# Graph layer kernel on one core: values and queries of layer 0 as seven block products

## The chip, the cores and the metric

The kernel runs on one NeuronCore of a Trainium2 chip. The core has five engines, each with its own instruction stream: TensorE (matmuls and its weight loads; PE and PEld in the profile), VectorE (DVE), ScalarE (ACT), GpSimd (POOL) and SyncE (SP), which here only starts transfers. They meet through semaphores. Matmul results land in PSUM, eight banks of 2 KB per partition; the rest of the working data is in SBUF, 128 partitions wide. The metric is the device time of one execution in microseconds (us), as the median of several runs.

## The reference

Two layers over 4096 rows of 512 features. Only the head of layer 0 is touched by the change:

```python
h = relu(layernorm(x))                       # 4096 x 512
q = h @ Wq.T + bq;  k = h @ Wk.T + bk;  v = h @ Wv.T + bv
a = q @ k.T / sqrt(512) + adj + adj
x = x + softmax(a) @ v
# layer 1: a graph attention with 8 heads on relu(layernorm(x)), and x + elu(...)
```

Everything is fp32 in layer 0. The kernel never forms k: q k.T is h (Wq.T Wk) h.T plus a bias term, so it forms A = Wq.T Wk once, then "queries" h A + c for each block of rows, and multiplies those with h.

## The kernel before, in words

*Stages.* In the profiled execution the projection runs from 0 to about 273 us, then the attention of layer 0 up to about 1.86 ms, a short preparation, and layer 1. In the attention stages matmuls are already written as seven products of half-size blocks (Strassen's scheme in Winograd's form) instead of eight: `product` and `weighted` with factors named A11 to A22, S1 to S4 (sums of blocks of h) and B11 to B22, T1 to T4 (sums of blocks of the other side). The projection before multiplies in the plain way.

*The projection* goes over eight blocks of 512 rows (NS = 8, `sb` in the code). For a block:

- `load_x` fetches four tiles of 128 rows; `normalize` (VectorE) takes means and variances, asks GpSimd for a power (`inverse_root`, L168), refines it in four small steps and scales the four tiles.
- `hidden` turns the block: 16 transposes on TensorE into two PSUM banks (tag `pt`), four activations on ScalarE (L411) into `hT`, then four sums on GpSimd into `hS` (L419 to L422; S1 to S4), and stores of both for the attention stage.
- `values_of`: for each of four tiles of 128 rows, four matmuls of 512 columns into one PSUM bank (L433), and one sum with the bias on VectorE into `v` (L437). Then per pair of tiles four GpSimd operations (L442 to L445) that make the sums T1, T2, T3 and T4 of `v`, T2 in place.
- `queries`: for each of four column blocks o of A, four matmuls of 512 columns into one bank (L459), one VectorE operation that adds c, scales by half_scale and reorders into `qs` (L463). Then four GpSimd sums (L472 to L475) and seven stores to `q_d`, in the order B21, B11, T1, T2, B22, T3, T4.

Both kinds of matmul take their bank from one tag, `mm`, with four banks.

*Order.* `seq` (`keep_in_program_order`) keeps every engine in the order in which the code names its instructions. In round sb that is: `normalize(sb + 1)`, `values_of(sb)`, `hidden(sb + 1)`, in round 2 `center_weights` (six VectorE operations, L252 to L254), in rounds 3 to 6 `weigh_weights` (four GpSimd products L260, each with a VectorE reduction L265), then `queries(sb)`. So on VectorE the sums of `values_of(sb)` stand behind `normalize(sb + 1)`, and on GpSimd the power of `normalize(sb + 1)` stands behind the query sums of round sb - 1. Round 0 is written out before the loop: loads of x, of Wv (L492), of Wq and Wk (`load_blocks`, L318), `normalize(0)`, `hidden(0)`, bias loads from ScalarE (L499, L500), eight VectorE transposes of Wq and Wk (L324), `values_of(0)`, `normalize(1)`, `attention_vectors` (small VectorE work for layer 1, L211 to L232), a GpSimd product of Wk with the bias (L507), 16 matmuls `pa` for A (L513) with ScalarE copies into `a_sb` (L517), the reduction to `c_sb` (L518), `hidden(1)`, `queries(0)`.

*Space.* `early` holds the 11 buffers of tag `qt` for query factors; `bv_sb` takes one during the projection. At round 6, `load_chunk(0)` loads seven.

Of the kernel before, what the change touches and what calls it, by code (L numbers as in the profile page):

```python
# [10 lines left out]
F32 = mybir.dt.float32  # L11
BF16 = mybir.dt.bfloat16
AF = mybir.ActivationFunctionType
ALU = mybir.AluOpType
# [65 lines left out]
def fast_path(  # L80
# [29 lines left out]
    def sources_of_rows(t):  # L110

        return t.rearrange("p (q c r) -> p c q r", c=SB, r=R)
# [195 lines left out]
    with tc.tile_pool(name="early", bufs=2) as early, tc.tile_pool(name="kv", bufs=1) as kv:  # L308
# [68 lines left out]
        with tc.tile_pool(name="proj_c", bufs=1) as pc, tc.tile_pool(  # L377
            name="proj", bufs=2
        ) as work, tc.tile_pool(name="proj_ps", bufs=2, space=PSUM) as psum:

            wv_sb = [
                pc.tile([P, D], F32, name=f"wv{k}_sb") for k in range(KC)
            ]
            a_sb = pc.tile([P, KC, D], F32, name="a_sb")
            c_sb = pc.tile([P, KC], F32, name="c_sb")
            bv_sb = early.tile([P, D], F32, name="bv_sb", tag="qt", bufs=11)
# [18 lines left out]
            def hidden(sb, xt):  # L405
# [20 lines left out]
                flat = "p a b c d -> p (a b c d)"  # L426
                seq(nc.sync.dma_start(out=s_d[sb].rearrange(flat), in_=sums.rearrange(flat)))

            def values_of(sb):
                for b in range(SB):  # L430
                    pv = psum.tile([P, 512], F32, name="pv", tag="mm", bufs=4)
                    for k in range(KC):
                        seq(nc.tensor.matmul(  # L433
                            pv, hidden_of[sb][0][:, k, ts(b, P)], wv_sb[k],
                            start=k == 0, stop=k == KC - 1,
                        ))
                    seq(nc.vector.tensor_add(v[:, sb * SB + b, :], pv, bv_sb))  # L437
                for pair in range(SB // 2):
                    one, two = v[:, sb * SB + 2 * pair, :], v[:, sb * SB + 2 * pair + 1, :]
                    b11, b12, b21, b22 = one[:, 0:H], one[:, H:D], two[:, 0:H], two[:, H:D]  # L440
                    t = early.tile([P, 3, H], F32, name="tv", tag="tv", bufs=2)
                    seq(nc.gpsimd.tensor_sub(t[:, 0], b12, b11))  # L442
                    seq(nc.gpsimd.tensor_sub(t[:, 1], b22, b12))
                    seq(nc.gpsimd.tensor_sub(b12, b22, t[:, 0]))
                    seq(nc.gpsimd.tensor_sub(t[:, 2], b21, b12))  # L445
                    seq(nc.sync.dma_start(
                        out=vt_d[sb * (SB // 2) + pair].rearrange("p f d -> p (f d)"),
                        in_=t.rearrange("p f d -> p (f d)"),
                    ))
# [3 lines left out]

            def queries(sb):
                qs = pc.tile([P, KC, GC], F32, name="qs", tag="qs", bufs=1)
                for o in range(KC):
                    pq = psum.tile([P, 512], F32, name="pq", tag="mm", bufs=4)
                    for k in range(KC):
                        seq(nc.tensor.matmul(  # L459
                            pq, a_sb[:, k, ts(o, P)], hidden_of[sb][0][:, k, :],  # L460
                            start=k == 0, stop=k == KC - 1,
                        ))
                    seq(nc.vector.tensor_scalar(  # L463
                        sources_of_rows(qs[:, o, :]), pq.rearrange("p (c q r) -> p c q r", c=SB, r=R),
                        c_sb[:, o : o + 1], half_scale, ALU.add, ALU.mult,
                    ))
                ts4 = prep.tile([P, SB, KC // 2, H], F32, name="ts4", tag="x1", bufs=1)
                t = [ts4[:, e] for e in range(4)]
                b = {f"{k + 1}{i + 1}": qs[:, 2 * k : 2 * k + 2, ts(i, H)]
                     for i in range(2) for k in range(2)}  # L470

                seq(nc.gpsimd.tensor_sub(t[0], b["12"], b["11"]))  # L472
                seq(nc.gpsimd.tensor_sub(t[1], b["22"], t[0]))
                seq(nc.gpsimd.tensor_sub(t[2], b["22"], b["12"]))
                seq(nc.gpsimd.tensor_sub(t[3], b["21"], t[1]))  # L475
                for f, name in enumerate(FACTORS):
                    seq(nc.sync.dma_start(
                        out=q_d[sb, :, f], in_=b[name[1:]] if name[0] == "B" else t[int(name[1]) - 1]
                    ))
# [9 lines left out]

            xts = {0: load_x(0)}  # L490
            for k in range(KC):
                seq(nc.sync.dma_start(out=wv_sb[k], in_=wvT[ts(k, P), :]))  # L492
            load_blocks(raw["q"], wqT)
            load_blocks(raw["k"], wkT)
            xts[1] = load_x(1)
            seq(nc.sync.dma_start(out=wk_rows, in_=wkT.rearrange("(k p) o -> p k o", p=P)))
            normalize(xts[0])
            hidden(0, xts.pop(0))
            seq(nc.scalar.dma_start(out=bv_sb, in_=bv[None, :].to_broadcast([P, D])))  # L499
# [8 lines left out]
                wk_rows, wk_rows, bq_sb.unsqueeze(1).to_broadcast([P, KC, D])  # L508
            ))
            for k in range(KC):  # L510
                pa_ps = psum.tile([P, 512], F32, name="pa", tag="mm", bufs=4)
                for c in range(SB):
                    seq(nc.tensor.matmul(  # L513
                        pa_ps, turned["q"][:, c, ts(k, P)], turned["k"][:, c, :],
                        start=c == 0, stop=c == SB - 1,
                    ))
                seq(nc.scalar.copy(a_sb[:, k, :], pa_ps))  # L517
            seq(nc.vector.tensor_reduce(c_sb, wk_rows, AX.X, ALU.add))  # L518
            xts[2] = load_x(2)
            hidden(1, xts[1])  # L520
            queries(0)
# [1223 lines left out]
```

## Time and profile before

| | |
|---|---|
| median of three runs | 3674.54 us (3672.04 to 3674.67) |
| the profiled execution's own time | 3674.76 us |
| its span, first to last instruction | 3672.7 us |
| mean granted TensorE clock | 0.988 of full |
| busy: TensorE / VectorE / GpSimd / ScalarE | 97% / 69% / 62% / 48% |
| projection stage | 0 to about 273 us |
| one round of it (95.16 to 125.03 us) | 29.87 us |

How to read the rows below: a line in order of time has start (us), duration (us), engine, line of the kernel, operation, output <- input (buffer numbers left out), shape, and xN for N merged instructions; in square brackets the time that the engine sat idle before it and what released it. PE matmul durations are pipelined: 592 ns is shown for a 512-column pass, while passes start 0.429 us apart, so times between starts are used. An fp32 matmul is recorded as two passes.

### The profile page before, as it was taken

The numbers are of one execution on the slowest core, as the hardware profiler recorded it, in microseconds if no ns is written. First come the engines' busy times: TensorE is split into PE (matmuls) and PEld (weight loads), VectorE is DVE, ScalarE is ACT, GpSimd is POOL, SyncE is SP. The second block draws the span as 40 slices with busy tenths as digits, with TensorE's granted clock in tenths as the row PEclk, the third lists the DMA queues.
The fourth block names the chain that finished last, engine by engine and source line by source line (L and its number), as shares of the span: only waits on it lengthen the run. The fifth ranks groups of instructions, "written<-read, shape, count | busy, mean of one in ns | idle before, by whom it ended". The sixth has DMA issues, their size and how long they took to land. (4 is left out here: it accounts for less than half of the span.)

```text
span 3672.7 us, 58831 instructions
## 1 busy us (share of the span) xinstructions
PE 3551.3 (97%) x21482; PEld 2084.0 (57%) x21482; DVE 2548.8 (69%) x4195; ACT 1745.0 (48%) x1541; POOL 2263.0 (62%) x1770
## 2 busy tenths in 40 slices
PE   8998999999999999999988799999999999999998
PEld 3447888888888888888866223322222223322332
DVE  5435565666666665656556678888888888888887
ACT  1000111111111111111123589998999999989997
POOL 4653445454545454444445568887888888877886
PEclk9999999999999999999999899999999999999999
DMA  6567788888888888888758987887787787778775
GB/s 213 180 207 203 230 242 239 238 242 244 237 234 250 237 237 243 241 249 232 217 143 207 214 220 211 211 212 201 211 209 212 203 213 204 209 198 214 211 210 151
DMA packets 667530, 796.85 MB, mean 217 GB/s; under 512 B 86816, under 2 KB 489696, under 8 KB 658016
## 3 DMA queue, kind: packets, MB, share of 16 engines
q1 hardware_dynamic: 655136, 759.64, 73.6%
q0 software_dynamic: 10704, 31.98, 4.8%
q8 instruction: 171, 2.80, 0.3%
q10 hardware_dynamic: 1392, 1.38, 0.1%
q14 instruction: 127, 1.04, 0.1%
HBM read 602.28 MB, written 182.71 MB: 214 GB/s over the span
## 5 line engine op out<-in xcount | busy, mean ns | idle before, releaser
L928 POOL TENSOR_TENSOR t<-t,g 128x1024 f32<-128x1024 f32 x512 | 1223.1, 2398 | 318.0 <-DVE t L922 242.4
L947 PE MATMUL acc<-t,nX 128*64 128x512 f32 x4096 | 1009.9, 609 | 0.0
L935 ACT ACTIVATE t<-t 128x2048 f32<-128x2048 f32 (+1 forms) x527 | 976.6, 1854 | 0.2 <-POOL t L928 0.2
L922 DVE SCALAR_TENSOR_TENSOR t<-u,at2m,r 128x512 f32<-128x512 f32 x1024 | 718.6, 743 | 209.3 <-issue 145.3
L597 ACT ACTIVATE aT<-aT 128x512 f32<-128x512 f32 x256 | 161.2, 630 | 1415.7 <-DVE aT L593 1415.7
L593 DVE TENSOR_TENSOR aT<-aT,XZ 128x256 f32<-128x256 f32 x896 | 352.9, 417 | 596.8 <-PE XZ L585 592.4
L931 DVE TENSOR_TENSOR t<-l,g 128x1024 f32<-128x1024 f32 x512 | 622.5, 1216 | 20.7 <-DMA g<-gT_d 16.7
L890 ACT ACTIVATE l<-l 128x1024 f32<-128x1024 f32 x512 | 516.5, 1009 | 149.4 <-PE l L884 101.5
L947 PEld LDWEIGHTS acc<-t,nX 128*64 128x64 f32 x4096 | 248.0, 136 | 458.3 <-issue 450.7
L585 PE MATMUL XZ<-qt,hS 128*128 128x256 f32 x2048 | 488.2, 382 | 9.6 <-DVE aT L593 9.6
L585 PEld LDWEIGHTS XZ<-qt,hS 128*128 128x128 f32 x2048 | 390.6, 191 | 64.1 <-DVE aT L593 11.1
L609 POOL TENSOR_TENSOR S<-aT 128x256 f32<-128x256 f32 x128 | 93.0, 726 | 525.8 <-ACT aT L597 525.8
L585 PE MATMUL XZ<-qt,hT 128*128 128x256 f32 x1536 | 374.3, 380 | 4.6 <-DVE aT L593 3.8
L621 POOL TENSOR_TENSOR total<-total,aT 128x256 f32<-128x256 f32 x360 | 326.5, 919 | 9.4
L585 PEld LDWEIGHTS XZ<-qt,hT 128*128 128x128 f32 x1536 | 291.3, 190 | 47.9 <-DVE aT L593 7.2
L874 PEld LDWEIGHTS <-z 6*128 6x128 bf16 x2048 | 52.4, 91 | 433.1 <-DVE t L922 350.2
L610 POOL TENSOR_TENSOR aT<-aT 128x256 f32<-128x256 f32 x128 | 93.0, 726 | 287.3 <-ACT aT L597 287.3
L636 PE MATMUL M<-v,aT 128*128 128x256 f32 x1024 | 263.0, 379 | 0.0
L636 PE MATMUL M<-tv,aT 128*128 128x256 f32 x1024 | 262.7, 379 | 0.0
L636 PE MATMUL M<-v,S 128*128 128x256 f32 x1024 | 242.0, 379 | 0.0
L577 DVE SCALAR_TENSOR_TENSOR gs<-ng,aT 128x512 f32<-128x512 bf16 x256 | 225.7, 882 | 8.8
L884 PE MATMUL l<-z_left,z 64*64 64x512 bf16 x2048 | 203.0, 383 | 26.8 <-DVE t L931 17.1
(178 smaller groups left out, 4372.0 us busy)
## 6 DMA issues: line engine op xcount, KB each, us to landing
g<-gT_d SPq DMA_DIRECT2D x128, 1024.0 KB
ag<-in_adj_dram SPq DMA_DIRECT2D x256, 256.0 KB
hS<-s_d SPq DMA_DIRECT2D x64, 1024.0 KB
gT_d<-gs SPq DMA_DIRECT2D x256, 256.0 KB
nb<-nT_d SPq DMA_DIRECT2D x128, 512.0 KB
nx<-nT_d SPq DMA_DIRECT2D x256, 256.0 KB
hT<-h_d SPq DMA_DIRECT2D x64, 768.0 KB
tv<-vt_d SPq DMA_DIRECT2D x128, 384.0 KB
```

The costliest lines, as they stand in the source:

```text
L577: seq(nc.vector.scalar_tensor_tensor(gs, ng, G_MASKED / NEG_BIG, aT, ALU.mult, ALU.add))
L585: seq(nc.tensor.matmul(out, a, b, start=start and k == 0, stop=k == 1, skip_group_check=not start,))
L593: seq(nc.vector.tensor_add(p, p, part))
L621: seq(nc.gpsimd.tensor_add(t, t, a))
L636: seq(nc.tensor.matmul(sums[ic][i][:, u, :], a[:, ts(u, P)], b, start=jt == 0 and u == 0, stop=jt == NB - 2, skip_group_check=u == 1,))
L884: seq(nc.tensor.matmul(lefts[n][ts(c, HD), r, :], loads[n // JB][2][ts(r, HD), jt % JB * P + c * HD :][:, :HD], groups[ic, hg]["z1_left"][ ...
L890: seq(nc.scalar.activation(lefts[n], lefts[n], AF.Relu, scale=4.0))
L922: seq(nc.vector.scalar_tensor_tensor(t[:, 2 + e, :], u4[:, e, :], at2m[:, jt, h : h + 1], right[e], ALU.max, ALU.add))
L928: seq(nc.gpsimd.tensor_mul(t[:, 2:4, :], t[:, 2:4, :], both_heads(n)))
L931: seq(nc.vector.tensor_mul(logits[n][:, 0:2, :], lefts.pop(n), both_heads(n)))
L935: seq(nc.scalar.activation(t, t, AF.Exp))
L947: seq(nc.tensor.matmul(grp["acc"][hf][ts(e, HD), :], nX[jt // SB][:, jt % SB, hg * HG + 2 * hf + e, :], t[:, hf + 2 * e, :], start=jt == 0 ...
```

## The change

The projections of values and of queries are written as seven products of half-size blocks, by the scheme that the attention stages use. A block of h (512 rows x 512 features) is cut into A11 to A22 by rows (even and odd tiles of 128, so the halves j) and by features (halves k); the sums S1 to S4 are those that `hidden` already makes for the attention stage. The weight (Wv, and A) is cut into B11 to B22. `weight_sums` forms T1, T3 and T4 of a weight in three new tiles and T2 in place of B12, with four GpSimd operations, once for each weight: for Wv right after the loads are issued, ahead of the first `normalize`; for A after the reduction to `c_sb`, ahead of `hidden(1)`.

`seven` runs four stages (`STAGES`). Each product is done in two halves u (values: tiles of 128 rows; queries: 128 output columns), and each half is a group of two matmuls of 256 columns. Tags X and Z have two banks each, one for each u. X is started once and accumulates X = A11 B11, then S2 T2, S3 T3 and A22 T4; Z is started anew in stages 0 and 1 and accumulates S4 B22 in stage 2. After every group VectorE reads the bank and adds it to the output's quarter: the first read of a quarter adds the bias, later ones add to what is there. Z of stage 0 with X of stage 0 gives quarter 11; Z of stage 1 starts quarter 22, X of stage 1 quarter 12; stage 2 completes 12 and 22; stage 3 gives 21. So a call has 28 matmuls of 256 columns and 14 VectorE operations of 256 columns, where it had 16 matmuls and 4 operations of 512. For queries, half_scale moves into `a_sb` (the ScalarE copy becomes a scaled one) and `c_sb` (one more small VectorE operation). The matmuls `pa` take their banks from X and Z in turn. The three tiles of sums of A come from the tag `qt`.

```diff
--- before.py
+++ after.py
@@ -378,9 +378,7 @@
             name="proj", bufs=2
         ) as work, tc.tile_pool(name="proj_ps", bufs=2, space=PSUM) as psum:
 
-            wv_sb = [
-                pc.tile([P, D], F32, name=f"wv{k}_sb") for k in range(KC)
-            ]
+            wv_sb = pc.tile([P, KC, D], F32, name="wv_sb")
             a_sb = pc.tile([P, KC, D], F32, name="a_sb")
             c_sb = pc.tile([P, KC], F32, name="c_sb")
             bv_sb = early.tile([P, D], F32, name="bv_sb", tag="qt", bufs=11)
@@ -426,15 +424,69 @@
                 flat = "p a b c d -> p (a b c d)"
                 seq(nc.sync.dma_start(out=s_d[sb].rearrange(flat), in_=sums.rearrange(flat)))
 
+            def weight_sums(w, tiles):
+
+                b11, b12, b21, b22 = [
+                    w[:, 2 * k : 2 * k + 2, ts(i, H)] for k in range(2) for i in range(2)
+                ]
+                t1, t3, t4 = tiles
+                seq(nc.gpsimd.tensor_sub(t1, b12, b11))
+                seq(nc.gpsimd.tensor_sub(t3, b22, b12))
+                seq(nc.gpsimd.tensor_sub(b12, b22, t1))
+                seq(nc.gpsimd.tensor_sub(t4, b21, b12))
+                return {"B11": b11, "B21": b21, "B22": b22, "T1": t1, "T2": b12, "T3": t3, "T4": t4}
+
+            def hidden_sides(sb):
+                h, sums = hidden_of[sb]
+                a = h.rearrange("p k (t j r) -> p k t j r", j=2, r=P)
+                sides = {f"A{j + 1}{k + 1}": a[:, 2 * k : 2 * k + 2, :, j, :]
+                         for j in range(2) for k in range(2)}
+                sides.update({f"S{i + 1}": sums[:, i] for i in range(4)})
+                return sides
+
+            STAGES = (
+                (("Z", "A12", "B21", True, "11"), ("X", "A11", "B11", True, "11")),
+                (("Z", "S1", "T1", True, "22"), ("X", "S2", "T2", False, "12")),
+                (("Z", "S4", "B22", False, "12"), ("X", "S3", "T3", False, "22")),
+                (("X", "A22", "T4", False, "21"),),
+            )
+
+            def seven(sides, weights, operands, out_of, add_bias):
+
+                seen = set()
+                banks = {}
+                for stage_ in STAGES:
+                    for u in range(2):
+                        for bank, a, b, start, to in stage_:
+                            if bank + str(u) not in banks or (bank == "Z" and start):
+                                banks[bank + str(u)] = psum.tile(
+                                    [P, 512], F32, name=bank, tag=bank, bufs=2
+                                )
+                            m = banks[bank + str(u)][:, 0:H]
+                            for k in range(2):
+                                one, two = operands(sides[a], weights[b], k, u)
+                                seq(nc.tensor.matmul(
+                                    m, one, two, start=start and k == 0, stop=k == 1,
+                                    skip_group_check=not start,
+                                ))
+                            o = out_of(to, u)
+                            if (to, u) in seen:
+                                m = m if len(o.shape) == 2 else m.rearrange("p (t q r) -> p t q r", t=2, r=R)
+                                seq(nc.vector.tensor_add(o, o, m))
+                            else:
+                                seen.add((to, u))
+                                add_bias(o, m, to, u)
+
             def values_of(sb):
-                for b in range(SB):
-                    pv = psum.tile([P, 512], F32, name="pv", tag="mm", bufs=4)
-                    for k in range(KC):
-                        seq(nc.tensor.matmul(
-                            pv, hidden_of[sb][0][:, k, ts(b, P)], wv_sb[k],
-                            start=k == 0, stop=k == KC - 1,
-                        ))
-                    seq(nc.vector.tensor_add(v[:, sb * SB + b, :], pv, bv_sb))
+
+                def add_bias(o, m, to, u):
+                    seq(nc.vector.tensor_add(o, m, bv_sb[:, ts(int(to[1]) - 1, H)]))
+
+                seven(
+                    hidden_sides(sb), wv, lambda a, b, k, u: (a[:, k, u, :], b[:, k, :]),
+                    lambda to, u: v[:, sb * SB + 2 * u + int(to[0]) - 1, ts(int(to[1]) - 1, H)],
+                    add_bias,
+                )
                 for pair in range(SB // 2):
                     one, two = v[:, sb * SB + 2 * pair, :], v[:, sb * SB + 2 * pair + 1, :]
                     b11, b12, b21, b22 = one[:, 0:H], one[:, H:D], two[:, 0:H], two[:, H:D]
@@ -453,17 +505,21 @@
 
             def queries(sb):
                 qs = pc.tile([P, KC, GC], F32, name="qs", tag="qs", bufs=1)
-                for o in range(KC):
-                    pq = psum.tile([P, 512], F32, name="pq", tag="mm", bufs=4)
-                    for k in range(KC):
-                        seq(nc.tensor.matmul(
-                            pq, a_sb[:, k, ts(o, P)], hidden_of[sb][0][:, k, :],
-                            start=k == 0, stop=k == KC - 1,
-                        ))
-                    seq(nc.vector.tensor_scalar(
-                        sources_of_rows(qs[:, o, :]), pq.rearrange("p (c q r) -> p c q r", c=SB, r=R),
-                        c_sb[:, o : o + 1], half_scale, ALU.add, ALU.mult,
+
+                def out_of(to, u):
+                    o = 2 * (int(to[1]) - 1) + u
+                    return qs[:, o, :].rearrange("p (q t j r) -> p j t q r", t=2, j=2, r=R)[:, int(to[0]) - 1]
+
+                def add_bias(o, m, to, u):
+                    n = 2 * (int(to[1]) - 1) + u
+                    seq(nc.vector.tensor_scalar_add(
+                        o, m.rearrange("p (t q r) -> p t q r", t=2, r=R), c_sb[:, n : n + 1]
                     ))
+
+                seven(
+                    hidden_sides(sb), wa, lambda a, b, k, u: (b[:, k, ts(u, P)], a[:, k]),
+                    out_of, add_bias,
+                )
                 ts4 = prep.tile([P, SB, KC // 2, H], F32, name="ts4", tag="x1", bufs=1)
                 t = [ts4[:, e] for e in range(4)]
                 b = {f"{k + 1}{i + 1}": qs[:, 2 * k : 2 * k + 2, ts(i, H)]
@@ -489,11 +545,14 @@
 
             xts = {0: load_x(0)}
             for k in range(KC):
-                seq(nc.sync.dma_start(out=wv_sb[k], in_=wvT[ts(k, P), :]))
+                seq(nc.sync.dma_start(out=wv_sb[:, k, :], in_=wvT[ts(k, P), :]))
             load_blocks(raw["q"], wqT)
             load_blocks(raw["k"], wkT)
             xts[1] = load_x(1)
             seq(nc.sync.dma_start(out=wk_rows, in_=wkT.rearrange("(k p) o -> p k o", p=P)))
+            wv = weight_sums(wv_sb, [
+                pc.tile([P, 2, H], F32, name=f"wvt{e}") for e in range(3)
+            ])
             normalize(xts[0])
             hidden(0, xts.pop(0))
             seq(nc.scalar.dma_start(out=bv_sb, in_=bv[None, :].to_broadcast([P, D])))
@@ -508,14 +567,19 @@
                 wk_rows, wk_rows, bq_sb.unsqueeze(1).to_broadcast([P, KC, D])
             ))
             for k in range(KC):
-                pa_ps = psum.tile([P, 512], F32, name="pa", tag="mm", bufs=4)
+                pa_ps = psum.tile([P, 512], F32, name="pa", tag="XZ"[k % 2], bufs=2)
                 for c in range(SB):
                     seq(nc.tensor.matmul(
                         pa_ps, turned["q"][:, c, ts(k, P)], turned["k"][:, c, :],
                         start=c == 0, stop=c == SB - 1,
                     ))
-                seq(nc.scalar.copy(a_sb[:, k, :], pa_ps))
+                seq(nc.scalar.activation(a_sb[:, k, :], pa_ps, AF.Identity, scale=half_scale))
             seq(nc.vector.tensor_reduce(c_sb, wk_rows, AX.X, ALU.add))
+            seq(nc.vector.tensor_scalar_mul(c_sb, c_sb, half_scale))
+            wa = weight_sums(a_sb, [
+                early.tile([P, GC], F32, name="at", tag="qt", bufs=11).rearrange("p (k c) -> p k c", k=2)
+                for _ in range(3)
+            ])
             xts[2] = load_x(2)
             hidden(1, xts[1])
             queries(0)
```

## The prediction, made before the result was known

> **What bounds the kernel now.** I read the page first, then the busy time by stretches over the first 400 us, because every edited line runs before 297 us, then the order of time of TensorE, VectorE and GpSimd in one block of the projection. Of the page:
>
> ```profile
> PE 3551.3 (97%) x21482; PEld 2084.0 (57%) x21482; DVE 2548.8 (69%) x4195; ACT 1745.0 (48%) x1541; POOL 2263.0 (62%) x1770
> ```
>
> TensorE is busy nearly throughout, so time that it saves or loses anywhere shows up in the total. The stretches of 50 us (busy time and instructions of each engine, then granted clock, DMA share, GB/s):
>
> ```profile
> 100.00:150.00 50.00, 49.24 (x139) 23.36 (x138) 24.16 (x48) 4.34 (x8) 33.18 (x34) 1.00 0.56 197
> ```
>
> In the projection TensorE works 49.2 of 50 us; VectorE has half its time free. One block, TensorE in order of time (start, duration, count):
>
> ```profile
> 95.16 13.90 PE L433 MATMUL pv<-wv_sb,hT 128*128 128x512 f32 x32
> 108.90 1.04 PE L410 MATMUL pt<-ident,xt 128*128 128x128 f32 x8
> 110.31 1.15 PE L410 MATMUL pt<-ident,xt 128*128 128x128 f32 x8 [0.38 <-ACT hT L411]
> 111.29 13.90 PE L459 MATMUL pq<-hT,a_sb 128*128 128x512 f32 x32
> 125.03 13.90 PE L433 MATMUL pv<-wv_sb,hT 128*128 128x512 f32 x32
> ```
>
> Each fp32 matmul is two passes: 32 passes take 13.74 us (111.29 to 125.03), 0.429 us each; the transposes between take 2.39. TensorE never waits here. But VectorE does its share late. At that block's start, VectorE, then GpSimd:
>
> ```profile
> 95.36 0.75 DVE L463 TENSOR_SCALAR qs<-pq,c_sb 128x512 f32<-128x512 f32 x1 [2.68 <-PE pq L459]
> ...
> 101.13 0.16 DVE L170 TENSOR_TENSOR hw<-hr 128x4 f32<-128x4 f32 x1 [1.13 <-POOL hr L168]
> ...
> 103.76 1.28 DVE L437 TENSOR_TENSOR v<-pv,bv_sb 128x512 f32<-128x512 f32 x2
> ```
> ```profile
> 96.26 1.27 POOL L473 TENSOR_TENSOR ts<-qs,ts 128x512 f32<-128x512 f32 x1 [5.67 <-DVE qs L463]
> 97.48 1.27 POOL L474 TENSOR_TENSOR ts<-qs 128x512 f32<-128x512 f32 x1
> 98.72 1.26 POOL L475 TENSOR_TENSOR ts<-qs,ts 128x512 f32<-128x512 f32 x1
> 100.08 1.02 POOL L168 TENSOR_TENSOR hr<-hv,mhalf 128x4 f32<-128x4 f32 x1
> ```
>
> The first sum into v comes 8.6 us after the previous queries ended (95.16), because VectorE first normalizes the next block, whose power (L168) stands on GpSimd behind the query sums. TensorE doesn't feel it: four banks of four 512-column matmuls hold all 13.7 us of the values. The same holds before queries in blocks 3 to 6 (values ended at 138.76), where VectorE waits for GpSimd's products L260:
>
> ```profile
> 147.80 0.42 DVE L265 TENSOR_REDUCE w_sb<-prod 128x4 f32<-128x256 f32 x1 [8.15 <-POOL prod L260]
> ...
> 150.19 2.23 DVE L463 TENSOR_SCALAR qs<-pq,c_sb 128x512 f32<-128x512 f32 x3
> ```
>
> The first query bank is read 9.0 us after its matmuls began (141.16). Lastly, what an idle TensorE costs:
>
> ```profile
> 32.64 16.77 PE L513 MATMUL pa<-v 128*128 128x512 f32 x32 [4.43 <-DVE v L437]
> ```
>
> The same 32 passes took 16.60 us (32.64 to 49.24) after 4.43 us of idling: 2.87 too many. The weight loads show the first ones at half pace until about 38.
>
> [...] the 128x256 sums with a PSUM operand (L593) take 0.417 us here[...].
>
> **The change part by part.**
>
> *Passes.* A call has 14 groups (seven products, two halves u) of 2 matmuls of 256 columns, 4 passes. In the attention stage passes of 256 columns start 0.2155 us apart (20 from 318.95 to 323.27, busy throughout). 56 x 0.2155 = 12.07 us against 13.74: 1.67 saved per call, 26.7 over 16 calls. Unlike there, moving rows of the queries come in two pieces of 128; [...] I take nothing, since the old moving rows were as long in bytes and no row shows a loss.
>
> *Run-ahead.* Four banks remain, X and Z with two each, but each takes one group of 0.86 us before it must be read. TensorE goes 4 x 0.86 = 3.44 us into a call and then needs VectorE's first sum. The order of VectorE's instructions in the changed program keeps normalize ahead of the values' 14 sums, and L265's reductions ahead of the queries' sums. Once flowing it keeps up: 14 x 0.42 = 5.9 us of VectorE in 12.07, and a bank has two or three groups (at least 0.86 us) to be read.
>
> *Values of blocks 1 to 6* (Q is the end of the queries before). The last query sum ends at Q+0.6. "21" comes only in the last stage, and it is part of both left halves of qs, so all four query sums now wait, where one was done early: 4 x 1.24 from Q+0.75 to Q+5.7. Power to Q+6.85; the small steps and normalization as in the trace (101.13 to 103.76, 2.6 us): first sum at Q+9.5, TensorE resumes at Q+9.95. Stall 6.5 us[...], so half clock: 10 remaining groups 8.62 + 2.87 = 11.5. Call: 21.4 against 13.74, +7.7; six times, **+46.2**.
>
> *Queries of blocks 3 to 6* (E is the values' end). GpSimd finishes the second pair of tv by about E+3.4, when hT is also there (L411 ended 3.2 after); hS 5.0 us (142.04 to 147.04), products and reductions 3.15 (147.04 to 150.19): first query sum at E+11.55, TensorE resumes at E+12.05 instead of E+5.8. Stall 6.2, again half clock: 2.39 + 3.44 + 6.2 + 11.5 = 23.5 against 16.1, +7.4; four times, **+29.6**.
>
> *Other calls.* Queries 1: -1.7. Queries 2: VectorE's weight centering (109.70 to 115.71, 6.0) costs a stall of 1.2: -0.5. Values and queries 7 have nothing ahead: **-3.3**. Sum with both: **-5.5**.
>
> *Start.* GpSimd's four wv sums (4 x 1.26) stand ahead of the first power and wait for wv, which by the queue's waits lands around 8.7: power at 13.1 instead of 7.5, everything behind it 5.6 later. SyncE's last two wk loads share DMA semaphores with bias loads issued by ScalarE behind hidden(0), so they slip too, but two go earlier: I put VectorE's wk transposes at 31 (29.5 before; between 28.5 and 34). All four stand ahead of the values' sums: first sum 33.5, TensorE, idle since 23.3, resumes at 33.9, values end at 45.4; the 16 matmuls pa, which began at 32.64 before, end at 59.1 instead of 49.2. VectorE: statistics to 49.6, power and the 4.5 us product of wk rows on GpSimd (VectorE's L170 was held 4.46 us beside it) to 55.2, normalization to 57.7, attention vectors 11.6 (46.58 to 58.13) to 69.3, bias reduction 2.3 and the new scaling: first query sum at 71.9. Queries 0 begin at 61.5, stall from 64.9 to 72.3, end at 83.8 against 65.2: **+18.6**. GpSimd's wa sums (done by 64) and hS(1) lie inside that stall.
>
> *End.* Query sums 1.24 later, last read 0.3 sooner: the store of B22, for which the attention stage's first VectorE instruction waits (5.26 us now), comes 0.7 later: **+0.7**. The weight tiles take three of eleven qt buffers, and seven are loaded: no new wait there.
>
> Sum: 46.2 + 29.6 - 5.5 + 18.6 + 0.7 = +89.6. On the profiled execution's 3674.76 (span 3672.7 and 2.1 around it), which agrees with the median of 3674.54: 3764.
>
> **Bounds of what no row shows.** Clock: twelve stalls (ten, and two at the start)[...]; I take the 2.87 measured. Strided query sums: the 512-wide evacuation took 0.75 against 0.69, so 0.45; at most 0.75, which would add 0.6 per query call (5 in all), at least 0.36. Start: wk's landing gives -2.5 to +3.
>
> **The rivals.**
> 1. *The clock holds.* [...] Against it: 4.43 us sufficed once. None dropping leaves 89.6 - 12 x 2.87 = +55: 3730.
> 2. *Longer chains.* GpSimd and VectorE hold each other up (L420 took 2.34 instead of 1.26 at 114.58), or wk is late: 1 us on each of 12 stalls and 5 at the start: 3781.
> 3. *TensorE's arithmetic alone*, faster: if the first sum of each call came within 3.44 us, all 26.7 would be kept, and 3648 result. It decides at the head of each late call: ten stalls may average 2.7 us before the saving is gone, so sums would be needed 6.1 us after the previous call's end; 8.6 is measured already before the change. Only another order on VectorE would give it.
> 4. *No difference*: stalls near 2.7 us, by the same measure.
>
> **How the numbers follow.** Mine 0.70, rival 1 in whole or large part 0.12, rival 2 0.13, rival 3 0.04, rival 4 0.01. The likeliest is 3764. From a clock that mostly holds to longer chains: 3735 to 3785. Slower 0.95, same 0.01, faster 0.04; 0.2%, 7 us, is about what the runs can tell from no change.
>
> **What would show it.** The projection should end near 363 instead of 273, with the attention's stretches unchanged. Right: passes of 256 columns 0.2155 apart in free flow and 0.43 after stalls; TensorE idle about 6.5 us before the fifth group of values, released by VectorE's sums, and 6.2 in queries 3 to 6; 10 us in values 0 and 7 in queries 0; granted clock near 0.8 in these stretches. Wrong: values' sums ahead of normalize, sums above 0.86 us (VectorE the bound), or passes above 0.25 us without a stall.

## The result, and the profile after

| | before | after |
|---|---|---|
| median of four runs, same chip | 3674.61 us (3672.04 to 3682.04) | 3758.6 us (3754.0 to 3767.33) |
| ratio after / before | | 1.023, 95% interval 1.021 to 1.025 |
| profiled execution: own time, span | 3674.76, 3672.7 us | 3767.33, 3765.6 us |
| first matmul of the attention stage starts at | 272.97 us | 363.03 us |
| from there to the end of the span | 3399.7 us | 3402.6 us |

The kernel became 84 us slower by the medians, and 92.6 us by the two profiled executions' own times, of which the one after was the longest of its four. The start of the first attention matmul separates the edited part from the rest: 90.06 of the 92.9 us by which the span grew arise ahead of it. The rest varies from run to run (3393 to 3422 us in the profiles of this document's kernels), so that start is the sharper measure, and it is used below beside the times.

The page of the kernel after: busy time of the engines, TensorE in 40 slices of 94 us, and the granted clock in the same slices.

```profile
PE 3552.2 (94%) x21866; PEld 2173.0 (58%) x21866; DVE 2606.6 (69%) x4356; ACT 1744.3 (46%) x1541; POOL 2273.7 (60%) x1778
...
PE   5767999999999999999998789999999999999998
...
PEclk8888999999999999999999899999999999999999
```

TensorE's busy sum is what it was (3551.3 before), although it has less to compute: passes at half clock take back about what the shorter products save (26.8 and 26.7 us, as worked out below and in the prediction). The first four slices are the projection: TensorE is busy there five to seven tenths of the time, and its clock is between 0.8 and 0.9 of full. A stretch of 50 us in the middle of it (busy time and instructions of each engine, then clock, DMA share, GB/s):

```profile
150.00:200.00 50.00, 35.57 (x148) 29.54 (x147) 24.54 (x57) 2.17 (x4) 24.38 (x25) 0.86 0.44 155
```

No engine is near full: TensorE works 35.6 of 50 us, VectorE and GpSimd under half. This is what engines look like that wait for each other in turn. TensorE in order of time, values of block 1 (L468 is the matmul in `seven`; x4 is one group):

```profile
91.50 1.03 PE L468 MATMUL X<-wv_sb,hT 128*128 128x256 f32 x4
98.94 2.04 PE L468 MATMUL Z<-wvt,hS 128*128 128x256 f32 x4 [6.41 <-DVE v L483]
100.78 1.91 PE L468 MATMUL X<-wv_sb,hS 128*128 128x256 f32 x4
102.48 1.44 PE L468 MATMUL Z<-wvt,hS 128*128 128x256 f32 x4
```

The fifth group has no bank until VectorE's first sum (L483) frees one. The fourth group started at 91.50 and could have been followed at 92.36; TensorE went on at 98.94, 6.58 us late. Then groups start 1.84 and 1.70 us apart, where 0.864 is their free pace. VectorE and GpSimd over the same time (L170 is the first of the four refining steps that wait for the power L168; L528 is the first of the four query sums):

```profile
89.12 0.48 DVE L515 TENSOR_SCALAR qs<-X,c_sb 128x256 f32<-128x256 f32 x1 [0.38 <-PE X L468]
...
95.75 0.16 DVE L170 TENSOR_TENSOR hw<-hr 128x4 f32<-128x4 f32 x1 [2.20 <-POOL hr L168]
...
98.37 0.42 DVE L483 TENSOR_TENSOR v<-Z,bv_sb 128x256 f32<-128x256 f32 x1
```
```profile
89.68 1.28 POOL L528 TENSOR_TENSOR ts<-qs 128x512 f32<-128x512 f32 x1 [16.67 <-DVE qs L515]
...
94.70 1.01 POOL L168 TENSOR_TENSOR hr<-hv,mhalf 128x4 f32<-128x4 f32 x1
```

All four query sums wait for the last read of the queries (89.12), the power waits for them, VectorE waits for the power, and the values' first sum stands behind the normalization. It comes 9.5 us after the queries ended (88.91). The queries of block 3, TensorE and VectorE (L265 is the last of four weight reductions):

```profile
186.54 1.03 PE L468 MATMUL X<-hT,a_sb 128*128 128x256 f32 x4
193.79 2.08 PE L468 MATMUL Z<-hS,at 128*128 128x256 f32 x4 [6.21 <-DVE qs L515]
```
```profile
192.92 0.42 DVE L265 TENSOR_REDUCE w_sb<-prod 128x4 f32<-128x256 f32 x1 [0.26 <-POOL prod L260]
193.26 0.47 DVE L515 TENSOR_SCALAR qs<-Z,c_sb 128x256 f32<-128x256 f32 x1
```

And the start: TensorE (values 0 go on; A's matmuls; queries 0 go on; queries 0 end), then GpSimd (two of Wv's four sums, and the first power behind them).

```profile
37.28 2.04 PE L468 MATMUL Z<-wvt,hS 128*128 128x256 f32 x4 [11.81 <-DVE v L483]
...
48.25 13.90 PE L572 MATMUL pa<-v 128*128 128x512 f32 x32
...
77.65 2.05 PE L468 MATMUL Z<-hS,at 128*128 128x256 f32 x4 [9.73 <-DVE qs L515]
...
88.91 1.03 PE L468 MATMUL Z<-wv_sb,hT 128*128 128x256 f32 x4
```
```profile
8.16 1.26 POOL L433 TENSOR_TENSOR wvt<-wv_sb 128x512 f32<-128x512 f32 x1 [6.86 <-DMA wv_sb<-in_wvT_dram]
10.62 1.26 POOL L434 TENSOR_TENSOR wvt<-wv_sb 128x512 f32<-128x512 f32 x1 [1.20 <-DMA wv_sb<-in_wvT_dram]
...
14.52 1.04 POOL L168 TENSOR_TENSOR hr<-hv,mhalf 128x4 f32<-128x4 f32 x1
```

The 90.06 us, part by part, from the starts of calls in the two traces:

| part | before | after | change |
|---|---|---|---|
| queries 0 end at | 65.30 | 88.91 | +23.6 |
| values 1 to 6, each | 13.74 | 20.3 to 20.9 | +42.2 |
| queries 3 to 6 with transposes, each | 16.13 | 23.5 | +29.4 |
| queries 1, queries 2, values 7, queries 7 up to the first attention matmul | | | -1.65, +0.05, -1.65, -1.91 |

The sum is +90.06. Of the last 1.91, 0.26 is a shorter wait just ahead of the attention (0.58 us, 0.84 before).

### The profile page after: what moved, and what is told of

It is laid out like the page before. It is cut to its first block, busy times and chain, and to the rows that moved or that the text cites. A ratio compares the mean times of both kernels' runs of the same rounds, so it can differ in the third digit from the quotient of the medians.

```text
span 3765.6 us, 59876 instructions
## 1 busy us (share of the span) xinstructions
PE 3552.2 (94%) x21866; PEld 2173.0 (58%) x21866; DVE 2606.6 (69%) x4356; ACT 1744.3 (46%) x1541; POOL 2273.7 (60%) x1778
```

## The experiments

My theory: TensorE may run only 3.44 us ahead of VectorE's first read, the first reads come 9 us or more into a call because of what stands ahead of them on VectorE and GpSimd, and each stall is followed by a time at half clock. The rivals: (A) VectorE's 14 sums a call, in place of 4, set the pace; (B) GpSimd's new or lengthened work is what is late; (C) the clock alone makes the loss. Each ratio below is against executions of the kernel before that ran in the same series, and each start of the first attention matmul is read from one profile.

### One projection at a time

The changed kernel with plain queries, and the changed kernel with plain values, each still on X and Z with two banks:

```diff
 # e1_values_only: in queries(sb)
-                seven(
-                    hidden_sides(sb), wa, lambda a, b, k, u: (b[:, k, ts(u, P)], a[:, k]),
-                    out_of, add_bias,
-                )
+                for o in range(KC):
+                    pq = psum.tile([P, 512], F32, name="pq", tag="XZ"[o % 2], bufs=2)
+                    for k in range(KC):
+                        seq(nc.tensor.matmul(
+                            pq, a_sb[:, k, ts(o, P)], hidden_of[sb][0][:, k, :],
+                            start=k == 0, stop=k == KC - 1,
+                        ))
...
 # e2_queries_only: in values_of(sb)
-                seven(
-                    hidden_sides(sb), wv, lambda a, b, k, u: (a[:, k, u, :], b[:, k, :]),
...
+                for b in range(SB):
+                    pv = psum.tile([P, 512], F32, name="pv", tag="XZ"[b % 2], bufs=2)
...
```

> Values by seven products, queries in the plain way (their four 512-column banks from X and Z in turn; no sums of A). Theory (late reads against a run-ahead of four groups, then half clock): the stalls in queries 0 and 3 to 6 vanish, because a plain call runs 13.7 us ahead; values 1 to 6 keep a stall of about 5.6 us and some 2.2 us at half clock. Start +12.8 against the kernel before, values 1 to 6 +6.2 each, values 7 -1.7: +48, so 3723 us, first product of the attention at 321 us (before 273, after 363). Rival A (VectorE's 14 small operations per call set the pace): half of the loss, values 7 slow too, about 3717 us with the same loss in all eight calls. Rival B (the GpSimd weight sums at the start are the loss): about 3700 us and no stalls after 90 us.

> Queries by seven products, values in the plain way. Theory: no stall in values 1 to 7; queries 3 to 6 stall about 6.3 us and run some 2.2 us longer at half clock, +7.3 each; queries 1 and 7 -1.7 each, queries 2 +0.1; queries 0 stall about 7.5 us, start +8.7. Sum +35: 3710 us, first product of the attention at 308 us. Rival A: all eight query calls lose alike, and queries 1 and 7 are no shorter than 13.7 us. Rival B: as the kernel before but for the first 75 us.

Values only: 3733.9 us, ratio 1.014 (1.005 to 1.024), first attention matmul at 322.29. Queries only: 3719.8 us, 1.011 (1.004 to 1.017), at 310.42. Both starts are within 3 us of what I expected. The two parts add up: 49.3 and 37.5 make 86.8 of the 90.06 us. TensorE with values only, in values 1 and in the queries after them:

```profile
86.28 2.05 PE L468 MATMUL Z<-wvt,hS 128*128 128x256 f32 x4 [5.55 <-DVE v L483]
...
99.90 13.90 PE L511 MATMUL pq<-hT,a_sb 128*128 128x512 f32 x32
```

The plain queries flow without a gap, although the same work stands ahead of their reads: four 512-column groups on four banks cover it. The stall of the values is 0.86 us shorter than in the changed kernel, because with plain queries one of the four GpSimd query sums no longer waits for the last read. With queries only, the same holds the other way round (values 3, then queries 3):

```profile
133.79 13.90 PE L484 MATMUL pv<-wv_sb,hT 128*128 128x512 f32 x32
...
159.57 2.05 PE L468 MATMUL Z<-hS,at 128*128 128x256 f32 x4 [6.03 <-DVE qs L514]
```

So each projection loses by itself, and neither needs the other to stall.

### The clock by itself

The changed kernel with matmuls of no use (their sum goes to a bank that nobody reads) put between the fourth and fifth group of each call that stalls: 14 each, 27 in values 0, 22 in queries 0.

```diff
-                for stage_ in STAGES:
+                for s_, stage_ in enumerate(STAGES):
+                    if s_ == 1 and spare:
+                        d = psum.tile([P, 512], F32, name="D", tag="D", bufs=1)
+                        for e in range(spare):
+                            one, two = operands(sides["A11"], weights["B11"], 0, 0)
+                            seq(nc.tensor.matmul(d[:, 0:H], one, two, start=e == 0, stop=e == spare - 1))
```

> The changed kernel with matmuls of no use (into a spare bank, never read) put into the stalls: 14 of 256 columns (6.0 us) ahead of the fifth group of values 1 to 6 and of queries 3 to 6, 27 in values 0, 22 in queries 0. They take the idling away but not the wait. Theory: the clock stays whole, the ten late calls lose their 2.2 us each and the start 5: -27, so 3731 us, first product of the attention at 336 us, and 256-column passes 0.2155 us apart behind every wait. Rival C (the clock is not in it; passes behind a wait are slow for another reason): no gain, 3758 us or more. Rival A: no gain.

Measured 3737.8 us, ratio 1.016 (1.009 to 1.022), first attention matmul at 336.22, as expected. TensorE in values 1:

```profile
87.57 6.21 PE L463 MATMUL D<-wv_sb,hT 128*128 128x256 f32 x28
94.15 1.10 PE L475 MATMUL Z<-wvt,hS 128*128 128x256 f32 x4 [0.38 <-DVE v L490]
95.09 1.03 PE L475 MATMUL X<-wv_sb,hS 128*128 128x256 f32 x4
```

With TensorE occupied, the groups after the wait start 0.94 and then 0.86 us apart, the free pace; the mean granted clock of the execution is 0.989, where it was 0.978. All twelve clock drops together cost 363.03 - 336.22 = 26.8 us, 2.23 each. The other 63 us remain with the clock held, so rival C accounts for under a third.

### Less run-ahead in the kernel before

The kernel before, not the changed one, with one and with two banks in place of four:

```diff
-                    pv = psum.tile([P, 512], F32, name="pv", tag="mm", bufs=4)
+                    pv = psum.tile([P, 512], F32, name="pv", tag="mm", bufs=1)   # bufs=2 in the second
 # the same for pq and pa
```

> The kernel before with one PSUM bank for values, queries and pa instead of four: plain products, but only 3.43 us of run-ahead, as in the changed kernel. Theory: values 1 to 6 stall about 5 us behind normalize, queries 3 to 6 about 6.4 us behind the reductions, each with half clock after it, and besides every bank waits 0.7 us for its read: values 1 to 6 +9.5 each, queries 3 to 6 +10.1, other calls +2 to +3, start +25; in all about +134: 3808 us, first product of the attention at about 407 us. Rivals A and B (VectorE's 14 operations, or GpSimd's weight sums, neither of which is here): only the bank waits, 16 x 2.8 = +45, 3719 us, no stall above 1 us.

> The kernel before with two banks instead of four for the 512-column projections: TensorE can run 2 x 4 x 0.429 = 6.87 us ahead of VectorE's first read. My theory (run-ahead against the lateness of the first read): values 1 to 6 stall 2.4 us each, queries 3 to 6 2.9 each, [...] the other calls not at all; at the start about +13 (values 0 wait for the k-transposes, queries 0 stall about 4.6 with one clock drop). Sum 6 x 2.4 + 4 x 2.9 + 13 = +39: about 3714 us, first attention product near 312 us instead of 272.97. Rival A (VectorE's number of sums is the pace; this kernel has as few sums as the one before): no loss, 3675. Rival C (the loss is the same whatever the stall's length, because it is the clock): as with one bank, about 3820.

One bank: 3821.5 us, ratio 1.038 (1.030 to 1.046), first attention matmul at 416.09. Two banks: 3730.2 us, 1.016 (1.012 to 1.019), at 326.90. Neither has any of the changed arithmetic, and both have their long stalls in the same calls as the changed kernel, released by the first reads. One bank, values of block 2:

```profile
137.63 6.57 PE L433 MATMUL pv<-wv_sb,hT 128*128 128x512 f32 x8 [4.63 <-DVE v L437]
144.99 3.70 PE L433 MATMUL pv<-wv_sb,hT 128*128 128x512 f32 x8 [0.78 <-DVE v L437]
```

Two banks, values of block 2 and of block 4:

```profile
121.93 8.83 PE L433 MATMUL pv<-wv_sb,hT 128*128 128x512 f32 x16 [2.31 <-DVE v L437]
130.59 1.04 PE L410 MATMUL pt<-ident,xt 128*128 128x128 f32 x8
```
```profile
194.89 7.13 PE L433 MATMUL pv<-wv_sb,hT 128*128 128x512 f32 x16 [2.30 <-DVE v L437]
```

The sizes of the stalls came out as the theory has them (2.31 for 2.4 in values, 2.79 for 2.9 in queries 3 to 6), and rival A isn't needed for such a loss: with four sums a call, it is there as soon as the run-ahead is short. (That the 14 sums add nothing to it is for the next experiments to show.) But my sum of +39 counted no clock drop after these ten stalls, and that was wrong. Eight of them were followed by one: 8.66 us from 121.93 to 130.59 where 6.87 is the free time, 1.8 lost, and 1.5 at the least. Two weren't, among them that of block 4 (7.13 in place of 8.83). That, 14 us in sum, is nearly all of the difference between 327, where the first attention matmul came, and 312.

### Another order

Three kernels that compute all that the changed kernel computes, with the same matmuls and banks, and move only VectorE's and GpSimd's work, with the loads of x that it needs. The first, in rounds 1 to 7: the normalization of the block after next and the weighing go in pieces between the sums (`fill` names what follows which group). The second, at the start alone. The third is both, with the normalization of block 2 also taken out of the way of values 1.

```diff
 # e6_rounds_reordered
-                if sb + 1 < NS:
-                    normalize(xts[sb + 1])
...
-                values_of(sb)
+                in_values = {5: [(stats, 0)], 7: [(stats, 1)], 9: [(stats, 2)], 11: [(stats, 3)]}
+                in_queries = {3: [(refine,)]}
+                in_queries.update({4 + b: [(scale, b)] for b in range(SB)})
+                values_of(sb, in_values, power)
...
-                    weigh_weights(sb - 3)
-                queries(sb)
+                        in_queries.setdefault(9 + n, []).append((weigh_reduce, k, e, g))
+                queries(sb, in_queries)
...
 # e7_start_reordered
+            normalize(xts[0])
             wv = weight_sums(wv_sb, [
                 pc.tile([P, 2, H], F32, name=f"wvt{e}") for e in range(3)
             ])
-            normalize(xts[0])
...
-            for name in ("q", "k"):
-                for c in range(SB):
-                    turn_blocks(turned[name][:, c, :], raw[name], c)
+            for c in range(SB):
+                turn_blocks(turned["q"][:, c, :], raw["q"], c)
             values_of(0)
+            for c in range(SB):
+                turn_blocks(turned["k"][:, c, :], raw["k"], c)
```

> The changed kernel with only the order of VectorE's and GpSimd's work in rounds 1 to 7 altered: nothing but v's sums stands ahead of the values' first sum, and nothing but the transposes' operands ahead of the queries'; the normalization of the block after next, the centering and the weighing go in pieces between the sums. The start is as in the changed kernel, and values 1 keep their stall. My theory: values 2 to 6 lose their stall and clock drop (-8.7 each, 20.87 to 12.1), queries 3 to 6 theirs (-9 each, 23.5 to 14.5), queries 2 1.4: -44 - 36 - 1 = about -80 against the changed kernel, so 3679 us, first attention product near 283. Rival A (14 sums of 0.42 with 128x256 pieces are too many for VectorE in any order): stalls stay in sum, TensorE's idling only moves into the calls, under -20, first product above 340. Rival B (GpSimd's hS and tv sums, which come before, are what is late): values lose their stall, queries keep theirs, about -44, near 319.

> The changed kernel with only the start altered: the four sums of wv on GpSimd come behind the first normalization, and the k-transposes behind the values of block 0. My theory: values 0 lose most of their 11.8 us idling, and queries 0 still idle behind the attention vectors: queries 0 end 12 to 20 us earlier than 88.9, the rest unchanged, 3739 to 3747 us, first attention product 343 to 351. If the start were bound by the landing of the loads alone, under 5 us would come back.

> Both of these together, with the normalization of block 2 also out of the way of values 1. My theory: every call of rounds 1 to 7 takes 56 x 0.2155 = 12.07 us plus 2.4 of transposes in the queries, the first attention product comes near 250 us (272.97 before the change), and the whole takes about 3651 us, 23 less than before the change: 0.994 of it. Rival A: VectorE, now filled between its sums, becomes the bound, calls take 13.7 or more, and the time is 3675 or above. If the clock, not the order, were the cause, calls would still run at half pace.

Rounds: 3703.1 us, ratio 1.008 (1.005 to 1.011), first attention matmul at 300.25, which is 62.8 us before the changed kernel's, where I expected 80. Start: 3748.3 us, 1.020 (1.017 to 1.024), at 350.96, 12.1 us earlier, at the low end of the 12 to 20 that I expected; its time is 1.3 us above the range. Both: 3681.7 us, 1.0023 (1.0013 to 1.0034), at 282.03; expected were 3651 and 250. The direction is the theory's: order alone returned 81 of 90 us. Values 1, 4 and 5 of the third kernel take 12.08 or 12.09 us with four statistics between their 14 sums, so VectorE has room, and rival A falls. (Values 2 and 3, 13.77 and 12.76 us, begin with slow passes after idling in the queries ahead of them.) Rival B falls for the most part in the rounds, since GpSimd's sums hS and tv are all still there; what is true of it there is the fourth query sum that now waits, 0.86 us of each stall of the values. At the start Wv's sums had to move. But the order that I chose had faults of its own. VectorE, TensorE and GpSimd in the queries of block 1 of the third kernel:

```profile
97.25 1.05 DVE L423 TENSOR_TENSOR hw<-hr 128x4 f32<-128x4 f32 x1
98.34 1.19 DVE L424 TENSOR_TENSOR hw<-hw,hv 128x4 f32<-128x4 f32 x1
99.57 1.19 DVE L425 TENSOR_SCALAR hw<-hw 128x4 f32<-128x4 f32 x1
```
```profile
101.41 1.13 PE L502 MATMUL Z<-hS,a_sb 128*128 128x256 f32 x4 [1.08 <-DVE qs L554]
```
```profile
97.02 1.27 POOL L451 TENSOR_TENSOR hS<-hS,hT 128x512 f32<-128x512 f32 x1
98.24 1.27 POOL L452 TENSOR_TENSOR hS<-hT 128x512 f32<-128x512 f32 x1
99.47 1.26 POOL L453 TENSOR_TENSOR hS<-hT,hS 128x512 f32<-128x512 f32 x1
```

Steps on four columns, 0.16 us each in the changed kernel's values (95.75 above), take 1.05 to 1.19 us here: each ends with the GpSimd operation beside it. The queries of blocks 1 to 5 lost 1.1 to 1.6 us of idling by this, those of blocks 1 and 2 another 2.1 to the centering in one piece. Queries 0 still idled 12.3 us behind the attention vectors (end at 78.78).

### The faults taken away

```diff
 # e9_queries_freed, from the third kernel
+                    in_values = {6: [(refine,)]}
+                    in_values.update({7 + b: [(scale, b)] for b in range(SB)})
...
+                    in_queries = {1 + 2 * b: [(stats, b)] for b in range(SB)}
+                    in_queries[8] = [(power,)]
...
+                    in_queries[9] = [(center_mean, sb - 1)]
+                    in_queries[12] = [(center_rest, sb - 1)]
...
 # start: ScalarE's small loads first; k-transposes between the sums of values 0; wk's product on VectorE;
 # hidden(1) ahead of the last quarter of pa; half of the attention vectors' work between the sums of queries 0
+            values_of(0, {
+                8 + c: [(turn_blocks, turned["k"][:, c, :], raw["k"], c)] for c in range(SB)
+            })
...
+            for k in range(KC):
+                if k == KC - 1:
+                    hidden(1, xts[1])
```

> The previous kernel once more, with what its trace shows taken away: the refinement of the power, whose three small steps were each held some 1.2 us beside GpSimd's hidden sums in the queries, and the scalings now stand in the next values, where GpSimd is idle; the statistics take their place in the queries; the centering is cut in two; at the start the small loads of ScalarE are issued first, the k-transposes stand between the sums of values 0, hidden(1) ahead of the last quarter of pa, wk's product with the bias on VectorE, and half of the attention vectors' work between the sums of queries 0. My theory: no call idles over 0.3 us; queries of rounds 1 to 7 take 14.48 us (16.13 before the change), values 12.07 (13.74), queries 0 end near 63 to 66 (65.3 before): first attention product 247 to 251 us, so 22 to 26 us less than before the change, about 3650 us, 0.993 to 0.994 of it. Rival A (VectorE, with all this between its sums, is the bound): calls stay above 13.5 us and the time at 3670 or more. Rival D (what the projection gains is given back in the attention stage, whose loads come from SyncE's queue later than the earlier start wants them): the first attention product comes near 249, but the whole stays above 3662.

Measured over six runs: 3650.8 us (3644.1 to 3655.1), beside 3670.6 for the kernel before; ratio 0.995 (0.993 to 0.997). TensorE, values 3, queries 3, and the first attention matmul:

```profile
119.15 1.03 PE L514 MATMUL Z<-wv_sb,hT 128*128 128x256 f32 x4
...
122.60 1.03 PE L514 MATMUL Z<-wvt,hS 128*128 128x256 f32 x4
...
131.23 1.04 PE L453 MATMUL pt<-ident,xt 128*128 128x128 f32 x8
...
145.72 1.03 PE L514 MATMUL Z<-wv_sb,hT 128*128 128x256 f32 x4
...
250.34 1.99 PE L724 MATMUL XZ<-qt,hT 128*128 128x256 f32 x8 [0.58 <-DVE qs L563]
```

The fifth group (122.60) follows the first after 3.45 us, without a wait; values take 12.08 us, transposes and queries 14.49. The first attention matmul stands 22.63 us before that of the kernel before. Queries 0 end at 65.14 (65.30 before the change), so 22.5 of it come from the 14 calls after them, 1.6 us each on average; values 1, queries 1 and queries 2 save a little less than the rest (12.59, 12.27 and 12.27 us). What follows the projection takes 3397.4 us of the span (3399.7 before), so there is no sign that anything was given back there. One thing did not come out: I expected no idling above 0.3 us, and at the start values 0 still wait 0.56 us, queries 0 0.35 and 1.44, both for the GpSimd sums of A.

This also bears on my third rival in the prediction, the faster outcome. The arithmetic's gain is real and reachable; what withholds it in the changed kernel is the order of the work around the products, and at the start also the engine that one of them (Wk with the bias) ran on. The plain products in this new order were not run. In rounds 1 to 7 the order could give them little, since TensorE idles there at most 0.38 us a round in the kernel before; the 4.43 us of idling at its start, and the 2.87 after it, might shrink.

## Why the prediction was right, and where its sizes were off

*Outcome.* Predicted 3764, measured 3758.6, within the range. At the first attention matmul the sum was +89.6 with 0.7 of it later, and +90.06 was measured. That the sum is so close is partly luck, as two terms were off in opposite directions: the start by +5.0, values 1 to 6 by -4.0.

*Passes.* 12.07 us a call was predicted, 12.08 and 12.09 measured in values 7 and queries 1, which have nothing late ahead of them. The moving rows in two pieces of 128 cost nothing.

*Run-ahead.* As put: TensorE halts after four groups in every late call. With two banks in the kernel before, the stall shrank as computed.

*Values 1 to 6, +46.2 predicted, +42.2 measured.* The chain was right: query sums, power, normalization, first sum at 98.37, which is 9.5 us after the queries' end, as predicted. The late time was 6.58 (6.5 predicted). What was mis-sized is the clock: 2.87 us taken from one earlier place; from 98.94 to 109.80 ten groups took 10.86 us where 8.64 is free, 2.2 lost.

*Queries 3 to 6, +29.6 predicted, +29.4 measured.* Stall and chain as predicted; ten groups from 193.79 to 205.02 took 11.23, so the clock cost 2.6 here, and the late time was 6.4 rather than 6.2.

*Other calls, -5.5 predicted, -4.9 measured (without the 0.26 just ahead of the attention).* The centering in queries 2 cost all of the saving (idle 1.43 us, as against 1.2).

*Start, +18.6 predicted, +23.6 measured.* This is the term that was mis-sized. Its first step, that Wv's sums stand ahead of the first power, was right, but 8.7 and four sums of 1.26 make 13.7, not the 13.1 that I wrote, and the second sum waited 1.20 us more for Wv, so the power came at 14.52. The step "VectorE's wk transposes at 31" failed by more: they came at 34.34, just beyond the bounds I had given it (28.5 to 34). VectorE, before and after (the releaser is inferred; the second row names the load that SyncE issued right behind those of wk):

```profile
29.52 2.49 DVE L324 STREAM_TRANSPOSE v<-v 128x512 f32<-128x512 f32 x4 [11.58 <-DMA v<-in_wkT_dram]
```
```profile
34.34 2.49 DVE L324 STREAM_TRANSPOSE v<-v 128x512 f32<-128x512 f32 x4 [13.63 <-DMA xt<-in_x_dram]
```

SyncE's queue in the first 40 us, before and after (waits in us in total, times, longest):

```profile
SPq L318 <- DMA bv_sb<-in_bv_dram: 4.0, 1, 4.0
```
```profile
SPq L318 <- DMA bv_sb<-in_bv_dram: 9.0, 1, 9.0
```

The loads of wk wait on a bias load that ScalarE issues behind `hidden(0)`: 9.0 us, where it was 4.0. Two of the four do go earlier, as I had taken it (11.64 and 15.58 us, 14.45 and 18.78 before), but the last one goes at 25.82 instead of 20.43, and the transposes come 4.8 us later with it. In the last kernel those small loads are issued first, and the transposes come at 29.04, paced only by where they were put. The third step, attention vectors in 11.6 us, took 13.0 (61.39 to 74.43), and rows of it are longer while GpSimd makes its sums of A and hS (these three took 0.68, 0.42 and 0.69 before). VectorE:

```profile
63.17 1.51 DVE L214 TENSOR_TENSOR a_sb<-a_sb,aln_sb 128x512 f32<-128x512 f32 x1
64.61 1.49 DVE L211 TENSOR_SCALAR a_sb<-a_sb 128x512 f32<-128x512 f32 x1
66.13 1.64 DVE L212 TENSOR_TENSOR v<-a_sb,bln_sb 128x512 f32<-128x512 f32 x1
```

In the order that I gave: the resumption of values 0 was 3.4 us later than predicted, that of queries 0 5.3, and the two clock drops cost 2.3 and 2.6 in place of 2.87.

*End, +0.7 predicted.* The first VectorE instruction of the attention stage came 6.4 us after the last projection matmul, 6.2 before: +0.2.

*Rivals.* That the clock holds is excluded by the 2.23 us a stall that the useless matmuls returned. Longer chains were real at the start, with just the 5 us that I had put there, and hardly anywhere else. The granted clock was to be near 0.8 and is 0.86 to 0.90 in these stretches; drops shorter than assumed go that way, but how much of it they make isn't worked out.

## What to carry to other kernels

Before cutting a product into smaller groups, set two numbers side by side: how long TensorE can run on the free banks (banks times the time of one group), and how late the first read comes after the previous call's end, from the trace. Here the first fell from 13.7 to 3.44 us against a lateness of 9, and a saving of 1.67 us a call turned into a loss of about 7. What brought the time back, and the saving with it, was to put nothing on the reading engine ahead of its first read, and the rest between later reads, where no other engine's work holds it up.

## What the runs showed of the hardware

*Short idling slows TensorE too, sometimes.* Eight of ten stalls of 2.3 to 2.8 us in the kernel with two banks were followed by 1.5 to 1.8 us lost, and two were not. The measured price of a drop lay between 1.5 and 3.1 us, and the length of the stall alone does not set it. A longer one was not dearer: 2.87 after 4.63 us of idling (one bank, 6.57 in place of 3.70), 2.2 after 6.41. And stalls of one length were not equally dear: with values by seven products only, values 1 to 6 each idle 5.55 us, and lose 2.6, 3.1, 1.7, 2.6, 3.1 and 1.7 us after it. Where they cost the same, TensorE resumes 109.1 to 109.2 us apart. What sets the price was not shown. For sizing, 2.2 us was the mean over twelve.

*A VectorE operation on four columns can last as long as the GpSimd operation beside it.* In the changed kernel one took 4.48 us beside GpSimd's product of Wk with the bias (4.53); in the third kernel others took 1.05 to 1.19 beside hidden sums (1.26 and 1.27); with GpSimd idle they take 0.16 (95.75 in the changed kernel). Of the three held rows above, two have two inputs (L423, L424) and the third has one (L425); why they were held was not shown. Two of the query sums with a PSUM operand took 0.48 and 0.42 us beside the same hidden sums (96.05 and 96.91 in the third kernel).
